# Layer normalization of two batches made from a transposed copy of x and broadcast rows of moments

## The chip, the cores and the metric

The kernel runs on one core of a Trainium2 chip, as one launch. The metric is device time in microseconds (us). The work of a core is spread over engines with an instruction queue each: TensorE (PE, matrix products and transposes), VectorE (DVE), ScalarE (ACT), GpSimd (POOL) and SyncE (SP), whose queue issues nearly all of this kernel's DMA transfers between DRAM and on-chip memory. Matrix results land in PSUM, everything else lives in SBUF; both have 128 partitions.

## What is computed

Two layers run over x, 4 batches of 512 rows with 256 columns, float32. Each has the same frame and its own mixer and feed-forward part:

```python
xn = _layernorm(x, axis=-1)
s = _L0_attn_ref(xn, ...)
g = _silu(_L0_ffn_ref(xn, L0_ffn_W1, L0_ffn_W2, L0_ffn_W3))
x = x + s * g
xn = _layernorm(x, axis=-1)
s = _L1_attn_ref(xn, L1_attn_qkv, L1_attn_o_proj, L1_attn_gamma, L1_attn_beta)
g = _silu(_L1_ffn_ref(xn, L1_ffn_W1, L1_ffn_W2, L1_ffn_W3))
x = x + s * g
```

`_layernorm` subtracts the mean of each row and divides by the root of its variance plus 1e-5. The first layer's mixer starts from a zero state, so it reduces to a matrix product, a root-mean-square normalization and a residual. The second layer's is causal attention with one head. The feed-forward part is

```python
up_gate = jnp.einsum('bsd,hd->bsh', x, W1)
up_lin = jnp.einsum('bsd,hd->bsh', x, W3)
hidden = jax.nn.silu(up_gate) * up_lin
hidden = fwht(hidden)
out = jnp.einsum('bsh,dh->bsd', hidden, W2)
```

with H = 1024 hidden columns; `fwht` is a Walsh-Hadamard transform of the hidden columns.

## The kernel before

**Products.** Every float32 operand of a product is split into a high part, which ACT casts (line 61), and a low part, which DVE subtracts (line 62). A product is then three: high by high, high by low, low by high (`mm3`, all issued at line 70). A contraction runs over partitions, so the products with xn need xn transposed: columns on partitions, rows along the free axis. The two halves of 128 columns are called k = 0 and 1.

**Stages of the first layer.** The loop from line 1014 goes over the four batches; the text calls its turns stages one to four, and their tiles carry f_0 to f_3. A stage is the feed-forward part of one batch (`ffn`, line 474): for each of 8 column blocks c, 24 products of 128x512 into two PSUM tiles `f_bgu` (`f_b` followed by the batch, from zero), silu on ACT (line 535), a multiply with the second tile on DVE (line 537, the gate product, `f_bh`), the split into `f_bhh` and `f_bhl`, and one block later 12 products of 128x256 with W2 into `f_bdn` (its parts are `w2h` and `w2l`; the transform is folded into them beforehand by `prep_w2`, whose products are `w2ps`).

**What runs beside a stage.** `Beside` (line 893) takes a list of tasks, made of steps, and spreads the steps over the 16 slots of a stage, in the order of the list. In the stage of batch b (from zero) the tasks are, in order:

- the gate of the batch before (`gate_all`, from stage two on): silu of `f_(b-1)dn`, times s, added to x;
- the mixer of this batch (`mixer`, line 725): products `o` of the transposed xn with a folded matrix, squares on ACT, then on DVE line 739, four scalings of `osb` and the sum at line 745;
- the layernorm of the next batch (`norm(0, b+1)`, line 438). `layernorm` makes statistics (four bn_stats, four bn_aggr, one addition on DVE, a power on POOL) and xn (four tensor_scalar). `transpose_half` (line 290) then has PE transpose four blocks of 128x128 for each k into a PSUM tile (`xt_btp`), and the split reads that tile: ACT casts the high part of 128x512, DVE subtracts the low one. The result, `xTs[0, b]`, is what the next stage's products and mixer read;
- preparation of the second layer: in stage two its W2 (`prep_w2`) and the attention weights (`prep_second`); in stages three and four `prep_s(q)`, line 327, for q = 0 to 3. It loads a block of weights (`sraw`, 512 KB on SP), makes four sums of it on DVE (`ssum`, 128x256 each), splits blocks and sums (128x768 and 128x1024) and writes them to DRAM, from where the second layer reads them.

Two batches of the second layer's normalization begin in these stages too: `norm(1, 0)` in stage three, between `prep_s(1)` and `prep_s(2)`, and parts of the first attention in stage four, ahead of `prep_s(3)`. `norm(1, b)` computes xn and the moments of xn (`moments`, line 256), has PE transpose the 8 columns of moments into rows (`mrp`), copies the rows on ACT, writes them to a DRAM tile (`there`) and reads them back broadcast over all partitions (`mrb`, [128, 2, 512]), both on SP. `Attention.xt` and `.scaled` (lines 759 and 780) use these rows: each row of the transposed tile has the mean row subtracted and is multiplied by the row of inverse deviations (`xf`, pieces of 128x512).

**Order.** In the stages a scheduler decides each engine's order from the order of the program, the dependences and explicit hints: `after(ins)` has what is issued in it stand behind instruction `ins`. `first["gate"]` is the last gate product so far, `first["scaled"]` the last tensor_scalar of the latest layernorm, `first["moments"]` the latest addition in `moments`; `line["last"]` is the last PE instruction. From the end of stage four on, PE's order is the program's: the last two `f_3dn` blocks stand behind `tq` (line 794, attention's query products, split into `tqh` and `tql`), then the second layer's first units with `v` (line 802), whose PSUM tile takes one of the three banks of the pool `ms`, which the transposes, `mrp`, `o`, `tq` and `w2ps` use in turn. SP carries the loads and stores in the order it is given, and an instruction that waits there holds all behind it.

**Buffers.** `t4` is a pool of ten 4 KB tiles per partition, shared by `osb`, `sraw`, `ssum`, `sp`, `mrb` and others; `x` has four slots, `xn` three, `xt` two.

Of the kernel before, what the change touches and what calls it, by code (L numbers as in the profile page):

```python
# [11 lines left out]
F32 = mybir.dt.float32  # L12
# [5 lines left out]
ALU = mybir.AluOpType  # L18
# [3 lines left out]
P = 128  # L22
D = 256
B = 4
S = 512
H = 1024
NH = H // P
NT = S // P
DS = 16
LN_EPS = 1e-5  # L30
# [5 lines left out]
def kernel(ctx: ExitStack, tc: tile.TileContext, a: dict, out: bass.AP):  # L36
    nc = tc.nc

    wp = ctx.enter_context(tc.tile_pool(name="weights", bufs=1))
    act = ctx.enter_context(tc.tile_pool(name="act", bufs=2))  # L40
    dram = ctx.enter_context(tc.tile_pool(name="dram", bufs=2, space=bass.MemoryType.DRAM))
    ps = ctx.enter_context(tc.tile_pool(name="ps", bufs=2, space=PSUM))

    def t4(name, shape, dt=F32):
        return act.tile(shape, dt, tag="t4", name=name, bufs=10)
# [10 lines left out]
    def psum(name, shape, tag="ms", bufs=3):  # L56
        return ps.tile(shape, F32, tag=tag, name=name, bufs=bufs)
# [8 lines left out]
    line = {"fixed": False, "last": None}  # L66
# [10 lines left out]
    def transpose(*args):  # L77
        return in_line(nc.tensor.transpose, *args)
# [15 lines left out]
    xs = {}  # L94
# [4 lines left out]
    def load_x(b, nt=NT, queues=(nc.sync,)):  # L99
        xs[b] = x_slot(f"x{b}", [P, NT, D])  # L100
        src = a["x"][b].rearrange("(t p) d -> p t d", p=P)
        for t in range(0, NT, nt):
            queue = queues[t // nt % len(queues)]
            queue.dma_start(xs[b][:, t : t + nt, :], src[:, t : t + nt, :])

    ident, had_f, mask = (wp.tile([P, P], F32, name=n) for n in ("ident", "had_f", "mask"))
# [146 lines left out]
        return hi, lo  # L253


    def moments(name, x, mr):

        st = act.tile([P, NT, 6], F32, tag="stats", name=f"{name}st", bufs=4)
        mv = act.tile([P, NT, 2], F32, tag="mv", name=f"{name}mv", bufs=4)
        for t in range(NT):  # L260
            nc.vector.bn_stats(st[:, t, :], x[:, t, :])
        for t in range(NT):
            nc.vector.bn_aggr(mv[:, t, :], st[:, t, :])
        nc.vector.tensor_copy(mr[:, 0, :], mv[:, :, 0])
        first["moments"] = nc.vector.tensor_scalar(mr[:, 1, :], mv[:, :, 1], LN_EPS, None, ALU.add)
        nc.gpsimd.tensor_tensor(mr[:, 1, :], mr[:, 1, :], mhalf, ALU.pow)

    def layernorm(name, x, y, groups=(NT,)):
# [38 lines left out]
    xns, xTs, mrs = {}, {}, {}  # L307

    def xt_pair(name):

        both = act.tile([P, 2, 2, S], F32R, tag="xt", name=name, bufs=2)
        return both[:, 0], both[:, 1]
# [14 lines left out]
    def prep_s(q):  # L327

        raw = t4(f"sraw{q}", [P, 4, D])
        nc.sync.dma_start(raw, a["w13_1"][q])  # L330
        yield
        sums = t4(f"ssum{q}", [P, 4, D])
        a11, a12, a22, a21 = (raw[:, i, :] for i in range(4))
        s1, s2, s3, s4 = (sums[:, i, :] for i in range(4))
        nc.vector.tensor_tensor(s1, a21, a22, ALU.add)
        nc.vector.tensor_tensor(s3, a11, a21, ALU.subtract)
        nc.vector.tensor_tensor(s2, s1, a11, ALU.subtract)
        nc.vector.tensor_tensor(s4, a12, s2, ALU.subtract)
        yield
        sdram[q] = there = [  # L340
            dram.tile([P, 7, D], F32, tag=f"s{i}", name=f"s{i}_{q}", bufs=4) for i in range(2)
        ]
        for at, n, src in ((0, 3, raw), (3, 4, sums)):
            parts = [t4(f"sp{at}_{i}_{q}", [P, n, D], F32R) for i in range(2)]
            split(src[:, :n, :], *parts)
            for i in range(2):
                nc.sync.dma_start(there[i][:, at : at + n, :], parts[i].bitcast(F32))
            yield
# [32 lines left out]
    def norm_first():  # L381
# [53 lines left out]
        first["norm"] = hi_, lo_  # L435
        yield

    def norm(layer, b):
        xn = act.tile([P, NT, D], F32, tag="xn", name=f"xn{layer}_{b}", bufs=3)
        xns[layer, b] = xn  # L440
        with after(first["gate"] if b > 1 - layer else None):
            first["scaled"] = layernorm(f"ln{layer}_{b}", xs[b], xn)
        yield
        if layer:


            mr = act.tile([P, 2, NT], F32, tag="mr", name=f"mr{b}", bufs=2)
            moments(f"ln2_{b}", xn, mr)
            yield
            o = psum(f"mrp{b}", [2 * NT, P], **DN[b == 0])  # L450
            transpose(o, mr.rearrange("p a t -> p (a t)"), ident)
            rows = act.tile([2 * NT, P], F32, tag="rows", name=f"rows{b}", bufs=1)
            with after(first["table"] if b else None):
                nc.scalar.copy(rows, o)
            there = dram.tile([2 * NT, P], F32, tag="rows", name=f"there{b}")
            nc.sync.dma_start(there, rows)
            mrb = t4(f"mrb{b}", [P, 2, S])
            nc.sync.dma_start(
                mrb, there.rearrange("(a t) p -> a (t p)", a=2).unsqueeze(0).to_broadcast([P, 2, S])
            )  # L460
            mrs[b] = mrb
            yield
            return
        hi, lo = xTs[0, b] = xt_pair(f"xt0_{b}")
        for k in range(2):
            o = transpose_half(f"xt0_{b}", xn, k)
            first["xt"] = line["last"]
            split(o, hi[:, k, :], lo[:, k, :])
            yield

    def after(ins):
        return tc.issue_after(ins.ins) if ins else nullcontext()
# [252 lines left out]
    def mixer(b):  # L725

        xn, xT, m = xns[0, b], xTs[0, b], first["m"]
        osb = t4(f"osb{b}", [P, NT, D])
        r = small(f"ssr{b}")
        junk = t2(f"junk{b}", [P, D])  # L730
        for i in range(2):
            o = psum(f"o0_{b}_{i}", [P, 2, D])
            for j in range(2):
                mm3(o[:, j, :], k_pairs(xT, sl(2 * i + j), m, ALLD))
            nc.scalar.copy(osb[:, 2 * i : 2 * i + 2, :], o)
            for t in (2 * i, 2 * i + 1):
                nc.scalar.activation(junk, osb[:, t, :], AF.Square, accum_out=r[:, t : t + 1])
            yield
        nc.vector.tensor_scalar(r, r, 1.0 / D, RMS_EPS, ALU.mult, ALU.add)
        nc.gpsimd.tensor_tensor(r, r, mhalf, ALU.pow)  # L740
        for t in range(NT):
            nc.vector.scalar_tensor_tensor(
                osb[:, t, :], osb[:, t, :], r[:, t : t + 1], nwb, ALU.mult, ALU.mult
            )
        nc.vector.tensor_tensor(xn, xn, osb, ALU.add)
        yield

    class Attention:
# [3 lines left out]
        def __init__(self, b):  # L752
            self.b, self.halves = b, []
# [171 lines left out]
    def call(f, *args):  # L925
        f(*args)
        yield


    NORM, MIXER, W2P = 3, 3, 12  # L930
# [27 lines left out]
    first = {"table": None}  # L958
# [52 lines left out]


    dn = None
    for b in range(B):
        tasks = []
        if b == 0:
            prep = prep_first()
            next(prep)
            tasks.append((prep, 12))
        if b:  # L1020
            tasks.append((call(gate_all, f"g0_{b - 1}", dn, xns[0, b - 1], xs[b - 1]), 1))
        tasks.append((mixer(b), MIXER))
        if b + 1 < B:
            if b:
                load_x(b + 1)
            if b == 2:
                tasks.append((prep_s(0), 4))
            tasks.append((norm(0, b + 1), NORM))
        if b == 0:
            early = w2_tile("early0"), w2_tile("early1")  # L1030
            spare = [
                [early[i][:, 2 * c : 2 * c + 2, :].rearrange("p a d -> p (a d)") for i in range(2)]
                for c in range(NH // 2)
            ]
        if b == 1:
            raw2_1 = load_w2(1)
            w2_1 = w2_tiles(1)
            tasks.append((prep_w2(1, raw2_1, w2_1, t4), W2P))
            tasks.append((prep_second(), 5))
        if b == 2:  # L1040
            tasks += [(prep_s(1), 4), (norm(1, 0), NORM), (prep_s(2), 4)]
        if b == 3:
            atts = [Attention(0)]
            at = atts[0]
            parts = run(at.xt_half, 0), run(at.xt_half, 1), at.xt, at.scaled, at.split_sums
            tasks += [(call(f), 1) for f in parts]
            norms = {1: norm(1, 1)}
            tasks.append((prep_s(3), 4))
        bg = Beside(*tasks)
        if b == 0:  # L1050
            dn = ffn("f0_0", xTs[0, 0], w13, w2, bg.slot, NH, spare, parts=2, behind=True)
        else:
            tail = [run(atts[0].tq, j) for j in range(2)] if b + 1 == B else []
            dn = ffn(f"f0_{b}", xTs[0, b], w13, w2, bg.slot, tail=tail)
        bg.finish()
# [36 lines left out]
    for b in range(B):  # L1092
        a, final = atts[b], b + 1 == B
# [113 lines left out]
```

## Time and profile before

| | |
|---|---|
| time, median of 3 runs | 358.37 us (358.14 to 358.87) |
| time of the profiled execution | 358.41 us |
| its span | 356.6 us |
| mean granted TensorE clock | 1.00 |
| busy: PE, DVE, ACT, POOL | 350.6, 287.1, 197.7, 20.8 us |
| instructions: PE, DVE, ACT, POOL | 2477, 598, 374, 22 |

The span is the time from the first to the last instruction that the profiler shows; the time of the execution has 1.8 us more around it. Stage one's products begin at 7.7 us, stage two's at 50.8, stage three's at 87.5, stage four's at 127.5, and the second layer starts at some 170.5. A busy engine is not an engine on the path: DVE and ACT are busy beside PE.

A line of a group or of a timeline gives the engine, the source line, the operation, the tile written and the tiles read, and the shapes; "x4" counts the instructions in it. Buffer numbers are left out of tile names, so the four batches' xn are all `xn`.

### The profile page before, as it was taken

What the parts mean: (1) busy time and instruction counts of PE and PEld (TensorE: products, weight loads), DVE (VectorE), ACT (ScalarE), POOL (GpSimd) and SP (SyncE); (2) the same over time, 40 slices, a digit from 0 to 9 for tenths busy, and PEclk for the clock granted to TensorE, in tenths of its full rate; (3) what the DMA queues carried; (4) which work ended last, traced back from release to release, by engine and by line L of the source; (5) the groups of instructions that cost most, each with busy time, mean ns of one, the idle gap of its engine ahead of it and who ended that gap; (6) DMA issues with size and microseconds to landing.
All of it is one profiled execution on the core that took longest, in us unless ns stands there. A gap on an engine that the chain in (4) does not pass through costs nothing.

```text
span 356.6 us, 6276 instructions
## 1 busy us (share of the span) xinstructions
PE 350.6 (98%) x2477; PEld 326.8 (92%) x2477; DVE 287.1 (81%) x598; ACT 197.7 (55%) x374; POOL 20.8 (6%) x22
## 2 busy tenths in 40 slices
PE   7999999999999999999999999999999999999995
PEld 6878998888988898888999999999999999999994
DVE  6899659998579938998887957989679897678646
ACT  4666166265463425674467755586555676556443
POOL 2000110300020110100110001100011000000000
PEclk9999999999999999999999999999999999999999
DMA  7935000301044306656257145661554635445401
GB/s 242 339 97 200 2 1 2 117 0 61 0 164 172 139 38 239 249 180 193 109 208 265 37 170 209 219 235 79 206 188 171 221 163 206 143 151 190 196 2 59
DMA packets 16284, 52.25 MB, mean 147 GB/s; under 512 B 1632, under 2 KB 7936, under 8 KB 16256
## 3 DMA queue, kind: packets, MB, share of 16 engines
q1 hardware_dynamic: 15968, 51.60, 40.5%
q8 instruction: 19, 0.31, 0.4%
q10 hardware_dynamic: 288, 0.26, 0.2%
q14 instruction: 9, 0.07, 0.1%
HBM read 42.40 MB, written 9.45 MB: 145 GB/s over the span
## 4 chain that ended last, share of the span: by engine, by line
PE 97%; DVE 1%; DMA 1%; ACT 0%; issue 0%
PE f_0dn L70 6%; PE f_1dn L70 6%; PE f_2dn L70 6%; PE f_0gu L70 6%; PE f_1gu L70 6%; PE f_2gu L70 6%; PE f_3gu L70 6%; PE f_3dn L70 6%; PE sc L70 4%; PE pv L70 4%; PE o L70 3%; PE v L70 3%; PE tq L70 3%; PE w2ps L70 1%; PE pt L70 1%; PE f_3gu1g L70 1%
## 5 line engine op out<-in xcount | busy, mean ns | idle before, releaser
L70 PE MATMUL f_3gu<-xt,w 128*128 128x512 f32 x96 | 25.0, 396 | 0.0
L70 PE MATMUL f_2gu<-xt,w 128*128 128x512 f32 x96 | 24.8, 395 | 0.0
L70 PE MATMUL f_1gu<-xt,w 128*128 128x512 f32 x96 | 24.8, 395 | 0.0
L70 PE MATMUL f_0gu<-xt,w 128*128 128x512 f32 (+1 forms) x108 | 24.3, 378 | 0.0
L70 PEld LDWEIGHTS f_0gu<-xt,w 128*128 128x128 f32 x108 | 18.4, 188 | 4.4 <-issue 1.0
L70 PEld LDWEIGHTS f_1gu<-xt,w 128*128 128x128 f32 x96 | 17.0, 188 | 3.1
L70 PEld LDWEIGHTS f_2gu<-xt,w 128*128 128x128 f32 x96 | 17.0, 188 | 3.0
L70 PEld LDWEIGHTS f_3gu<-xt,w 128*128 128x128 f32 x96 | 17.0, 188 | 2.9
L61 ACT CAST f_2hh<-f_2h 128x512 fp32r<-128x512 f32 x16 | 10.0, 622 | 15.4 <-DVE f_2h L537 12.3
L70 PE MATMUL f_3dn<-w2l,f_3hh 128*128 128x256 f32 x64 | 17.7, 281 | 0.0
L70 PE MATMUL f_3dn<-w2h,f_3hh 128*128 128x256 f32 x64 | 17.7, 281 | 0.0
L70 PE MATMUL f_1dn<-w2l,f_1hh 128*128 128x256 f32 x64 | 17.7, 281 | 0.0
L70 PE MATMUL f_2dn<-w2h,f_2hh 128*128 128x256 f32 x64 | 17.7, 282 | 0.0
L70 PE MATMUL f_1dn<-w2h,f_1hh 128*128 128x256 f32 x64 | 17.6, 280 | 0.0
L70 PE MATMUL f_2dn<-w2l,f_2hh 128*128 128x256 f32 x64 | 17.6, 280 | 0.0
L70 PE MATMUL f_3dn<-w2h,f_3hl 128*128 128x256 f32 x64 | 17.0, 281 | 0.0
L70 PE MATMUL f_1dn<-w2h,f_1hl 128*128 128x256 f32 x64 | 17.0, 281 | 0.0
L70 PE MATMUL f_2dn<-w2h,f_2hl 128*128 128x256 f32 x64 | 16.7, 281 | 0.0
L61 ACT CAST f_3hh<-f_3h 128x512 fp32r<-128x512 f32 (+1 forms) x17 | 10.0, 594 | 10.3 <-DVE f_3h L537 6.1
L61 ACT CAST f_1hh<-f_1h 128x512 fp32r<-128x512 f32 x16 | 9.9, 621 | 9.7 <-DVE f_1h L537 6.6
L62 DVE TENSOR_TENSOR f_2hl<-f_2h,f_2hh 128x512 fp32r<-128x512 f32 x16 | 10.9, 684 | 4.5 <-ACT f_2hh L61 4.5
L62 DVE TENSOR_TENSOR f_3hl<-f_3h,f_3hh 128x512 fp32r<-128x512 f32 (+1 forms) x17 | 11.0, 654 | 3.7 <-ACT f_3hh L61 3.6
(487 smaller groups left out, 1146.1 us busy)
## 6 DMA issues: line engine op xcount, KB each, us to landing
sw<-s SPq DMA_DIRECT2D x32, 896.0 KB, 5.8
s<-sp SPq DMA_DIRECT2D x8, 512.0 KB, 4.1
s<-sp SPq DMA_DIRECT2D x8, 384.0 KB, 2.8
w2raw<-in_w SPq DMA_DIRECT2D x4, 512.0 KB, 4.8
sraw<-in_w SPq DMA_DIRECT2D x4, 512.0 KB, 4.2
mrb<-there SPq DMA_DIRECT2D x4, 512.0 KB, 3.7
w13raw<-in_w SPq DMA_DIRECT2D x3, 512.0 KB, 6.2
x<-in_x SPq DMA_DIRECT2D x3, 512.0 KB, 3.5
```

The costliest lines, as they stand in the source:

```text
L61: h = nc.scalar.copy(hi, src)
L62: return h, engine.tensor_tensor(lo, src, hi.bitcast(F32), ALU.subtract)
L70: ins = call(*args, **kwargs)
```

## The change

The layernorm of the third and the fourth batch in the first layer goes another way. A class `FromTransposed` holds its three parts, for b = 2 and 3:

- `begin`, the last task of stage one for the third batch and of stage two for the fourth: loads x of the batch, a second copy of it that the host has laid out transposed (`xT2`, `xT3`, [128, 2, 512]), and makes the moments on DVE and POOL;
- `rows`, in the stage ahead of the batch's own (stage two for the third batch, stage three for the fourth), directly behind the gate of the batch before: PE's transpose of the moments' 8 columns, the copy of the rows, the write to DRAM and the broadcast read;
- `steps`, in the place of `norm(0, b)`: xn by four tensor_scalar as before, since the mixer and the residual need it; then the transposed xn, from the transposed x by a subtraction of the mean row and a multiplication by the row of inverse deviations, each one DVE instruction of 128x1024 whose row operand is broadcast over k; the high part by one ACT cast of 128x1024, and the low part by one DVE subtraction of 128x1024, in place of the PE transposes and the two splits of 128x512 from PSUM.

The write and the broadcast read are taken out of `norm` into `spread`, which both use. `norm(0, 1)` and `norm(1, 0)` change a hint: they now stand behind `first["gate"]` too, where they had no hint. `moments` can leave `first["moments"]` as it is.

```diff
--- before.py
+++ after.py
@@ -253,7 +253,7 @@
         return hi, lo
 
 
-    def moments(name, x, mr):
+    def moments(name, x, mr, pin=True):
 
         st = act.tile([P, NT, 6], F32, tag="stats", name=f"{name}st", bufs=4)
         mv = act.tile([P, NT, 2], F32, tag="mv", name=f"{name}mv", bufs=4)
@@ -262,7 +262,9 @@
         for t in range(NT):
             nc.vector.bn_aggr(mv[:, t, :], st[:, t, :])
         nc.vector.tensor_copy(mr[:, 0, :], mv[:, :, 0])
-        first["moments"] = nc.vector.tensor_scalar(mr[:, 1, :], mv[:, :, 1], LN_EPS, None, ALU.add)
+        ins = nc.vector.tensor_scalar(mr[:, 1, :], mv[:, :, 1], LN_EPS, None, ALU.add)
+        if pin:
+            first["moments"] = ins
         nc.gpsimd.tensor_tensor(mr[:, 1, :], mr[:, 1, :], mhalf, ALU.pow)
 
     def layernorm(name, x, y, groups=(NT,)):
@@ -435,10 +437,67 @@
         first["norm"] = hi_, lo_
         yield
 
+    def spread(name, rows):
+
+        there = dram.tile([2 * NT, P], F32, tag="rows", name=f"there{name}")
+        nc.sync.dma_start(there, rows)
+        mrb = t4(f"mrb{name}", [P, 2, S])
+        nc.sync.dma_start(
+            mrb, there.rearrange("(a t) p -> a (t p)", a=2).unsqueeze(0).to_broadcast([P, 2, S])
+        )
+        return mrb
+
+    class FromTransposed:
+
+        def __init__(self, b):
+            self.b = b
+
+        def begin(self):
+            b = self.b
+            load_x(b)
+            self.raw = t4(f"xTraw{b}", [P, 2, S])
+            nc.sync.dma_start(self.raw, a[f"xT{b}"])
+            self.mr = act.tile([P, 2, NT], F32, tag="mr", name=f"mr0_{b}", bufs=2)
+            with after(first["scaled"] if b == 2 else first["gate"]):
+                moments(f"ln0_{b}", xs[b], self.mr, pin=False)
+            yield
+
+        def rows(self):
+            b = self.b
+            o = psum(f"mrp0_{b}", [2 * NT, P])
+            with after(line["last"]):
+                transpose(o, self.mr.rearrange("p a t -> p (a t)"), ident)
+            rows = act.tile([2 * NT, P], F32, tag="rows", name=f"rows0_{b}", bufs=1)
+            nc.scalar.copy(rows, o)
+            self.mrb = spread(f"0_{b}", rows)
+
+        def steps(self):
+            b, mr = self.b, self.mr
+            xns[0, b] = xn = act.tile([P, NT, D], F32, tag="xn", name=f"xn0_{b}", bufs=3)
+            with after(first["gate"]):
+                for t in range(NT):
+                    nc.vector.tensor_scalar(
+                        xn[:, t, :], xs[b][:, t, :], mr[:, 0, t : t + 1], mr[:, 1, t : t + 1],
+                        ALU.subtract, ALU.mult,
+                    )
+            yield
+            hi, lo = xTs[0, b] = xt_pair(f"xt0_{b}")
+            raw = self.raw
+            for i, op in enumerate((ALU.subtract, ALU.mult)):
+                row = self.mrb[:, i, :].unsqueeze(1).to_broadcast([P, 2, S])
+                with after(first["gate"]):
+                    nc.vector.tensor_tensor(raw, raw, row, op)
+            nc.scalar.copy(hi, raw)
+            yield
+            nc.vector.tensor_tensor(lo, raw, hi.bitcast(F32), ALU.subtract)
+            yield
+
     def norm(layer, b):
         xn = act.tile([P, NT, D], F32, tag="xn", name=f"xn{layer}_{b}", bufs=3)
         xns[layer, b] = xn
-        with after(first["gate"] if b > 1 - layer else None):
+        with after(first["gate"] if b or layer else None):
             first["scaled"] = layernorm(f"ln{layer}_{b}", xs[b], xn)
         yield
         if layer:
@@ -452,13 +511,7 @@
             rows = act.tile([2 * NT, P], F32, tag="rows", name=f"rows{b}", bufs=1)
             with after(first["table"] if b else None):
                 nc.scalar.copy(rows, o)
-            there = dram.tile([2 * NT, P], F32, tag="rows", name=f"there{b}")
-            nc.sync.dma_start(there, rows)
-            mrb = t4(f"mrb{b}", [P, 2, S])
-            nc.sync.dma_start(
-                mrb, there.rearrange("(a t) p -> a (t p)", a=2).unsqueeze(0).to_broadcast([P, 2, S])
-            )
-            mrs[b] = mrb
+            mrs[b] = spread(b, rows)
             yield
             return
         hi, lo = xTs[0, b] = xt_pair(f"xt0_{b}")
@@ -1011,6 +1064,7 @@
 
 
     dn = None
+    others = {b: FromTransposed(b) for b in (2, 3)}
     for b in range(B):
         tasks = []
         if b == 0:
@@ -1019,13 +1073,15 @@
             tasks.append((prep, 12))
         if b:
             tasks.append((call(gate_all, f"g0_{b - 1}", dn, xns[0, b - 1], xs[b - 1]), 1))
+            if b + 1 in others:
+                tasks.append((call(others[b + 1].rows), 0))
         tasks.append((mixer(b), MIXER))
         if b + 1 < B:
-            if b:
+            if b and b + 1 not in others:
                 load_x(b + 1)
             if b == 2:
                 tasks.append((prep_s(0), 4))
-            tasks.append((norm(0, b + 1), NORM))
+            tasks.append((others[b + 1].steps() if b + 1 in others else norm(0, b + 1), NORM))
         if b == 0:
             early = w2_tile("early0"), w2_tile("early1")
             spare = [
@@ -1046,6 +1102,8 @@
             tasks += [(call(f), 1) for f in parts]
             norms = {1: norm(1, 1)}
             tasks.append((prep_s(3), 4))
+        if b + 2 in others:
+            tasks.append((others[b + 2].begin(), 0))
         bg = Beside(*tasks)
         if b == 0:
             dn = ffn("f0_0", xTs[0, 0], w13, w2, bg.slot, NH, spare, parts=2, behind=True)
@@ -1174,6 +1232,8 @@
     flat = lambda n: v[f"L0_attn_{n}"].reshape(4, P, DS)
     arrays = {
         "x": v["L0_attn_x"],
+        "xT2": v["L0_attn_x"][2].T.reshape(2, P, S).transpose(1, 0, 2),
+        "xT3": v["L0_attn_x"][3].T.reshape(2, P, S).transpose(1, 0, 2),
         "ident": np.eye(P, dtype=np.float32),
         "hadamard": (_sylvester(P) / np.sqrt(H)).astype(np.float32),
         "mask": np.where(np.tril(np.ones((P, P), bool)), 0.0, NEG).astype(np.float32),
```

## The prediction

> **What bounds the kernel now.** I read the page first, for who is busy and who ends the chain of waits:
>
> ```profile
> span 356.6 us, 6276 instructions
> ...
> PE 350.6 (98%) x2477; PEld 326.8 (92%) x2477; DVE 287.1 (81%) x598; ACT 197.7 (55%) x374; POOL 20.8 (6%) x22
> ...
> PE 97%; DVE 1%; DMA 1%; ACT 0%; issue 0%
> ```
>
> PE is the whole chain, and the list of waits shows PE waiting for another engine only at the start (1.5 and 0.4 us). So a product taken off PE is worth its pitch (start to start), and any new PE wait costs its full length. The profiled execution took 358.41 us (the median of the runs is 358.37): span 356.6 and 1.8 around it. My sum starts from 358.41.
>
> Second, PE's timeline around the removed transposes, here the fourth batch's (columns: start, duration):
>
> ```profile
> 119.59 0.38 PE L70 MATMUL xt_3tp<-ident,xn 128*128 128x128 f32 x2
> 119.73 0.36 PE L70 MATMUL f_2dn<-w2h,f_2hh 128*128 128x256 f32 x1
> 119.93 0.28 PE L70 MATMUL f_2dn<-w2l,f_2hh 128*128 128x256 f32 x1
> ...
> 120.29 0.82 PE L70 MATMUL xt_3tp<-ident,xn 128*128 128x128 f32 x6
> 120.86 1.41 PE L70 MATMUL f_2gu<-xt,w 128*128 128x512 f32 x5
> 122.11 0.28 PE L70 MATMUL f_2dn<-w2h,f_2hl 128*128 128x256 f32 x1
> ```
>
> Starts matter here, not durations: two transposes hold PE 0.14 us, six hold it 0.57, and the product behind each group takes longer than its like (0.20 against 0.12; five wide ones 1.25 against 5 x 0.232 = 1.16).
>
> Third, how full DVE is, by stage (columns: window, its us, DVE busy and count, PE clock, DMA share, GB/s), since DVE gets the new work:
>
> ```profile
> 57.00:84.00 27.00, 26.70 (x52) 1.00 0.18 59
> 84.00:104.00 20.00, 12.59 (x21) 1.00 0.07 27
> 104.00:125.70 21.70, 21.40 (x60) 1.00 0.47 171
> 125.70:133.80 8.10, 1.99 (x4) 1.00 0.11 43
> 143.50:169.40 25.90, 23.93 (x49) 1.00 0.61 201
> ```
>
> DVE is full in three stretches, with holes of some 7 and 6 us between them. Fourth, DVE and the SP queue in the places where something could become late:
>
> ```profile
> 70.84 1.22 DVE L745 TENSOR_TENSOR xn<-xn,osb 128x1024 f32<-128x1024 f32 x1
> 73.18 0.69 DVE L62 TENSOR_TENSOR f_1hl<-f_1h,f_1hh 128x512 fp32r<-128x512 f32 x1
> 167.15 0.69 DVE L62 TENSOR_TENSOR tql<-tq,tqh 128x512 fp32r<-128x512 f32 x1 [0.46 <-ACT tqh L61]
> 167.91 0.66 DVE L62 TENSOR_TENSOR f_3hl<-f_3h,f_3hh 128x512 fp32r<-128x512 f32 x1
> ```
>
> ```profile
> 80.91 0.33 SPq L330 DMA_DIRECT2D sraw<-in_w  x1
> ...
> 129.94 0.33 SPq L456 DMA_DIRECT2D there<-rows  x1
> 131.17 0.34 SPq L458 DMA_DIRECT2D mrb<-there  x1
> 131.57 0.42 SPq L330 DMA_DIRECT2D sraw<-in_w  x1
> ...
> 136.54 0.43 DVE L335 TENSOR_TENSOR ssum<-sraw 128x256 f32<-128x256 f32 x1 [0.38 <-DMA sraw<-in_w]
> ```
>
> The write of rows lands within 1.23 us, mrb holds the queue 0.40, and the sraw behind it took 4.9 us to reach DVE.
>
> **PE: what goes and what comes.** Fourth batch: 0.14 + 0.57 + 0.08 + 0.09 = 0.88. Third batch, by the same reading at 71.88 to 74.62: 0.14 + 0.57 + 0.07 + 0.09 = 0.87. Each batch gains one 8-column transpose of moments: the mrp at 129.36 and the slower o product behind it cost 0.10 together. Net -1.75 + 0.20 = **-1.55 us**. Every PE instruction ahead of a late one moves up too, so the lead must be given back before anything is lost.
>
> A duration tempts here: the Trainium skill ("TensorE: Matmul & The Clock Gate", Part 4: PE-mode transpose) gives about 275 ns for a transpose in a kernel's context. The row's duration, 272 ns, agrees, but the pitch is 95 ns; by 275 ns the 16 would be worth 4.4 us, an estimate from the page, and the verdict below would turn round.
>
> **DVE, ACT, POOL per batch.** New on DVE: two tensor_tensor of 128x1024 over two SBUF tiles, 1.13 us of pitch each (the row at 70.84, followed by one at 71.97). A broadcast operand is not in the trace at this width; bounds are 1.13 and 2 x 0.60 = 1.20 (two 128x512 pieces, as xf<-xf,mrb at 0.60); I take 1.13. The final subtract is one of 1.13 instead of two of 0.60. The moments (4 stats 1.31, 4 aggregates 0.32, small ones 0.15) move one batch ahead, into the holes at 44 and 88 us, at no cost there: that work ran in full stretches before. ACT: one cast of 1.05 for two of 0.59, and a copy of rows of 0.25; ACT is 55% busy. POOL's power moves with the moments, long before its reader. Two x^T loads of 512 KB and two mrb transfers run where the DMA share is 0.07 to 0.31, hidden. The earlier pin of the second batch's layernorm in stage one falls in a stretch where DVE then idles 5.07 us (before L739): nothing.
>
> **First new wait: column block 3 of stage two.** In the built order of DVE, between f_1h0 and the f_1hl of column block 3, new are: a gate add 0.60, subtract 1.13, multiply 1.13, second w2l as well as the first 1.20, last subtract 1.13: 5.19. Gone from there: stats 1.31, aggregates 0.32, one small 0.07: 1.70. f_1h0 itself starts earlier (PE's order now finishes f_1gu0 without o products between: 14 wide pitches after 50.8, plus silu 0.60, gives 54.9 for 56.09). So f_1hl ends at 73.86 + 5.19 - 1.70 - 1.19 + 0.4 (it waits for ACT's f_1hh0 behind the new rows copy) = 76.6. PE read it at 76.48; now -0.87 + 0.10 for the transposes and +0.46 for a w2ps pair moved ahead: 76.2. With its high half, cast just before, I take **+0.65** (bounds 0 and 1.2, the latter if f_1h0 is not early).
>
> **Second and third: SP's order.** sraw (prep_s) now stands behind there, mrb of the fourth batch. Its transpose of rows comes after f_1dn's last product and 18 f_2gu products: 95.74 + 1.40 = 97.1. Copy and ACT's queue 0.6, there 1.23, mrb 0.40, landing 4.2 to 4.9: DVE gets sraw0 at 103.6 to 104.3 where it read it at 98.27. DVE idles in that hole, and the queue up to the moments of layer two (13 x 0.60, 6 x 1.13, 2 x 0.87, 8 x 0.33, osb 1.58, two xn 2.60, stats 2.62, small 0.85 = 26.6) ends near 130.6, for 125.7. (These prices reproduce before's own 104.36 to 125.71 to 0.1 us.) The row transpose mrp0 stands in PE's new order after f_3gu2's tenth product: 141.67 - 36 x 0.118 + 0.93 - 0.9 (PE's lead) = 137.4, where it ran at 129.36. Then sraw2 is issued at 139.6 instead of 131.57 and usable at 139.6 + 4.9 = 144.5 instead of 136.5. The five-step sums of prep_s(2) (3.3 us) fall out of a hole into the last full stretch.
>
> From 144.5 DVE has, up to the last f_3hl: 18 x 0.60, 12 x 0.33, 2 x 0.87, 3 x 1.13, osb 1.58, stats 1.31, small 0.23 = 23.05, and 2.0 of waits as before's stretch had: 169.55. PE wants it at 169.38 - 0.9 = 168.5: **+1.15**. Behind it, now ahead of tql: 0.56 of small ones, ACT's cast of sums (1.0 waited), 1.13, xn 1.30, two gate products 1.20, tql 0.68: it ends at 175.4, for 167.84. v's second half takes the PSUM bank that tql frees; PE reached it at 173.39, now 173.39 - 0.9 + 1.15 = 173.6: **+1.8**. Behind it in PE's fixed order everything waits.
>
> The Trainium skill ("DMA: Bandwidth & Descriptors", Anatomy of one DMA) puts about 2.0 us of fixed cost on a transfer, where the write of rows here was followed after 1.23. By 2.0 sraw2 would come 0.8 later and the sum be 0.8 higher, an estimate; the row is of this very transfer, so it decides.
>
> Sum: -1.55 + 0.65 + 1.15 + 1.8 = +2.05; 358.41 + 2.05 = **360.5 us**.
>
> **Rivals.** (a) The holes absorb all: 358.41 - 1.55 = 356.9. It needs tql no more than 4.0 us later than 167.84 (173.39 - 1.55 - 167.84); I get 7.5, so sraw2 would have to be usable by 141. For it: PE never waited before, with 2.6 us to spare at f_1hl and 5.5 at v. Against: the SP order. 10%. (b) Only the wait in stage two comes, the tail stays hidden: 358.41 - 1.55 + 0.65 = 357.5. Same condition on tql, at 3.4 us more given the lead that is left. 6%. (c) Only part of the tail: sraw2 lands after 4.2 and DVE's waits are shorter by 1: 358.41 - 1.55 + 0.65 + 0 + 1.2 = 358.7. 8%. (d) More: transfers or POOL's power (1.01 to 1.91 in its rows) slower beside the fuller DVE, prep_s late by another 2 us, which comes through whole: 362.5. 16%. That the change does not do what it says is excluded by the built order: 16 transposes are gone, two row transposes there. The forecast keeps 60%.
>
> **Range and chances.** A difference of 0.2% (0.7 us) is about what can be told here from none. Low end: between (c) and (a) with the unknown 0 to 1.2 of stage two, 358.6; high end (d), 362.6. Slower by over 0.2% (above 359.1): forecast, (d) and a little of (c): 0.80. Within: most of (c) and half of (b): 0.09. Faster: (a), the rest of (b): 0.11.
>
> **What would show it.** Eight transposes less in each of two stages, PE about 0.8 us ahead at f_2gu's start; tensor_tensor of 128x1024 on raw at 1.2 us; sraw's first issue near 99 and third near 140; DVE idle just before both; PE idle some 0.65 at f_1dn near 76, and 1 to 3 us in all at f_3dn and v near 169 to 175, released by DVE; layer two otherwise unchanged. Wrong if PE shows no wait at v, or if sraw's third issue comes before 136.

## The result and the profile after

The changed kernel takes 361.23 us (median of 6 runs, 360.86 to 361.84) against 358.34 for the kernel before: a ratio of 1.0079, interval 1.0068 to 1.0091, so 2.9 us slower. The profiled execution took 360.86, 2.45 more than the 358.41 of the one before; the traces below explain those 2.45. The profiled run was the fastest of the six, and what the other five lost beyond it is in no trace.

The page of the changed kernel, the lines on spans, engines and the chain that ended last:

```profile
span 359.1 us, 6272 instructions
...
PE 350.6 (98%) x2463; PEld 325.3 (91%) x2463; DVE 291.1 (81%) x602; ACT 198.4 (55%) x374; POOL 18.8 (5%) x22
...
PE 93%; DVE 4%; ACT 1%; issue 0%; DVEq 0%
```

PE has 14 instructions fewer, as the change says, but the chain is no longer all PE: 4% of it is DVE. PE's list of waits for other engines names three that weren't there (us in all, times, the longest):

```profile
PE v L70 <- DVE tql L62: 1.6, 1, 1.6
...
PE f_3dn L70 <- DVE f_3hl L62: 0.7, 1, 0.7
PE f_1dn L70 <- DVE f_1hl L62: 0.2, 1, 0.2
```

The list shows only what is left after the modelled end of the product before. The starts say more. PE's timeline at the three places:

```profile
72.88 1.55 PE L70 MATMUL f_1gu<-xt,w 128*128 128x512 f32 x6
74.49 0.39 PE L70 MATMUL f_1dn<-w2h,f_1hh 128*128 128x256 f32 x1
74.72 0.28 PE L70 MATMUL f_1dn<-w2l,f_1hh 128*128 128x256 f32 x1
...
75.06 1.58 PE L70 MATMUL f_1gu<-xt,w 128*128 128x512 f32 x6
76.83 0.38 PE L70 MATMUL f_1dn<-w2h,f_1hl 128*128 128x256 f32 x1 [0.19 <-DVE f_1hl L62]
77.05 0.28 PE L70 MATMUL f_1dn<-w2h,f_1hh 128*128 128x256 f32 x1
...
168.50 0.28 PE L70 MATMUL f_3dn<-w2l,f_3hh 128*128 128x256 f32 x1
169.51 0.38 PE L70 MATMUL f_3dn<-w2h,f_3hl 128*128 128x256 f32 x1 [0.72 <-DVE f_3hl L62]
169.73 0.28 PE L70 MATMUL f_3dn<-w2h,f_3hh 128*128 128x256 f32 x1
...
172.93 0.87 PE L70 MATMUL f_0gu0z<-tb,sw 128*128 128x256 f32 x6
175.41 0.50 PE L70 MATMUL v<-wvoh,xgh 128*128 128x256 f32 x2 [1.62 <-DVE tql L62]
```

Six wide products take 6 x 0.232 = 1.39, so the two starts in stage two come 0.22 and 0.38 late; after 168.50 the next was due at 168.62 and began 0.89 later; after 172.93 plus 6 x 0.118 it was due at 173.64 and began 1.77 later. Each first product after a wait also held PE 0.22 to 0.23 (74.49 to 74.72, 76.83 to 77.05, 169.51 to 169.73) where its like hold it 0.12: a wait costs its length and about 0.1 more.

DVE by the same windows as in the prediction:

```profile
57.00:84.00 27.00, 25.64 (x42) 1.00 0.26 79
84.00:104.00 20.00, 13.04 (x27) 1.00 0.16 53
104.00:125.70 21.70, 20.99 (x41) 1.00 0.47 171
125.70:133.80 8.10, 6.55 (x21) 1.00 0.16 65
...
143.50:169.40 25.90, 23.34 (x47) 1.00 0.67 221
```

The hole behind stage three's full stretch is mostly filled: 6.55 us busy between 125.7 and 133.8, for 1.99 before. DVE idles later instead, 3.87 us up to 142.52 and 1.32 up to 144.53, when the load comes. DVE's and SP's timelines where things became late:

```profile
69.68 1.22 DVE L491 TENSOR_TENSOR xTraw<-xTraw,mrb 128x1024 f32<-128x1024 f32 x1
70.82 0.68 DVE L590 TENSOR_TENSOR f_1h<-f_1h,f_1gu 128x512 f32<-128x512 f32 x1
...
76.09 0.69 DVE L62 TENSOR_TENSOR f_1hl<-f_1h,f_1hh 128x512 fp32r<-128x512 f32 x1
...
104.71 0.43 DVE L337 TENSOR_TENSOR ssum<-sraw 128x256 f32<-128x256 f32 x1 [1.15 <-DMA sraw<-in_w]
...
131.74 0.16 DVE L265 TENSOR_SCALAR mr<-ln_0mv 128x4 f32<-128x4 f32 x1
...
144.53 0.42 DVE L337 TENSOR_TENSOR ssum<-sraw 128x256 f32<-128x256 f32 x1 [1.32 <-DMA sraw<-in_w]
...
168.80 0.65 DVE L62 TENSOR_TENSOR f_3hl<-f_3h,f_3hh 128x512 fp32r<-128x512 f32 x1
...
172.17 1.38 DVE L286 TENSOR_SCALAR xn<-x,ln_1mv,ln_1r 128x256 f32<-128x256 f32 x4
173.47 1.29 DVE L767 TENSOR_TENSOR g_3g<-g_3g,xn 128x512 f32<-128x512 f32 x2
174.67 0.68 DVE L62 TENSOR_TENSOR tql<-tq,tqh 128x512 fp32r<-128x512 f32 x1
```

```profile
98.15 0.29 SPq L443 DMA_DIRECT2D there<-rows  x1
99.42 0.33 SPq L445 DMA_DIRECT2D mrb<-there  x1
99.80 0.42 SPq L332 DMA_DIRECT2D sraw<-in_w  x1
...
137.98 0.28 SPq L443 DMA_DIRECT2D there<-rows  x1
139.20 0.32 SPq L445 DMA_DIRECT2D mrb<-there  x1
139.57 0.43 SPq L332 DMA_DIRECT2D sraw<-in_w  x1
```

The load for prep_s(0) left SP at 99.80 for 80.91, the one for prep_s(2) at 139.57 for 131.57, and DVE got them at 104.71 and 144.53, each after an idle wait. The last `f_3hl` ends at 169.45 (168.57 before) and the first `tql` at 175.35 (167.84 before), behind the four xn and the two gate products that DVE did after it in the kernel before. The write of rows that holds the second load back waits for PE, not for DVE: DVE has the moments of norm(1, 0) ready at 131.90 and POOL their power at 133.05, but PE comes to their transpose only at 137.39, where it stands in PE's built order behind 34 products of `f_3gu` (behind six in the kernel before, at 129.36).

### The profile page after: what moved, and what is told of

Read it like the earlier page. It is cut to its first block, busy times and chain, and to the rows that moved or that the text cites. A ratio compares the mean times of both kernels' runs of the same rounds, so it can differ in the third digit from the quotient of the medians.

```text
span 359.1 us, 6272 instructions
## 1 busy us (share of the span) xinstructions
PE 350.6 (98%) x2463; PEld 325.3 (91%) x2463; DVE 291.1 (81%) x602; ACT 198.4 (55%) x374; POOL 18.8 (5%) x22
## 4 chain that ended last, share of the span: by engine, by line
PE 93%; DVE 4%; ACT 1%; issue 0%; DVEq 0%
PE f_0dn L70 6%; PE f_2dn L70 6%; PE f_0gu L70 6%; PE f_3gu L70 6%; PE f_2gu L70 6%; PE f_1dn L70 6%; PE f_1gu L70 5%; PE f_3dn L70 5%; PE sc L70 4%; PE pv L70 4%; PE o L70 3%; PE v L70 3%; PE tq L70 2%; PE warm L70 1%; PE pt L70 1%; PE w2ps L70 1%
## 5 line engine op out<-in xcount | busy, mean ns | idle before, releaser
L70 PE MATMUL f_0dn<-w2h,f_0hh 128*128 128x256 f32 x48 | 13.6, 283 | 0.0
```

Source lines behind the costliest of these rows:

```text
L70: ins = call(*args, **kwargs)
```

## The experiments

Each is compared with the kernel before on the same chip. "Net" is the shift of PE's last product against the kernel before in the two profiled executions, less the shift that the execution already had when the first stage's products began (these starts differ by up to 0.6 from one execution to the next).

**Both weight loads ahead on SP.** Nothing else is changed:

```diff
+            if b == 2:
+                s0 = prep_s(0)
+                tasks.append((call(next, s0), 1))
             if b + 1 in others:
                 tasks.append((call(others[b + 1].rows), 0))
...
-                tasks.append((prep_s(0), 4))
+                tasks.append((s0, 3))
...
-            tasks += [(prep_s(1), 4), (norm(1, 0), NORM), (prep_s(2), 4)]
+            s2 = prep_s(2)
+            tasks += [(prep_s(1), 4), (call(next, s2), 1), (norm(1, 0), NORM), (s2, 3)]
```

> The changed kernel with two loads moved ahead on SP and nothing else: the weights of prep_s(0) are loaded before the rows of the fourth batch are spread, those of prep_s(2) before norm(1, 0) is issued. DVE, ACT and PE do the same instructions. Theory (the sums of prep_s come late because their loads stand behind the two writes and broadcast reads of rows, and fall into the last full stretch of DVE): DVE reads sraw of q = 0 near 86 and of q = 2 before 128, PE's waits at the last f_3dn (0.88 by pitch) and at v (1.78) both go, with the 0.1 that the first product after each loses; stage two's wait stays. PE's lead over before stands at 0.76 ahead of the tail, so 358.4 - 0.76 = 357.6, at most 358.0. Rival (DVE simply has too much to do in all): the same work is there, both waits stay, 361.2. Rival (the added transfers take bandwidth): they are all still there, 360 or more.

Measured: 357.98 (357.57 to 358.61, 10 runs), ratio 0.9991 (0.9982 to 1.0001); net -0.6. SP's and DVE's timelines of this kernel:

```profile
81.58 0.33 SPq L332 DMA_DIRECT2D sraw<-in_w  x1
98.73 0.29 SPq L443 DMA_DIRECT2D there<-rows  x1
...
121.20 0.38 SPq L332 DMA_DIRECT2D sraw<-in_w  x1
...
138.76 0.28 SPq L443 DMA_DIRECT2D there<-rows  x1
```

```profile
100.63 0.41 DVE L337 TENSOR_TENSOR ssum<-sraw 128x256 f32<-128x256 f32 x1
...
169.21 1.25 DVE L62 TENSOR_TENSOR tql<-tq,tqh 128x512 fp32r<-128x512 f32 x2
```

The sums begin at 100.63 and 138.12, in DVE's holes again (98.27 and 136.54 in the kernel before), though not near 86 and before 128 as expected. With the same 602 instructions on DVE, both low parts of tq now end by 170.46, and PE's only new wait is stage two's. 3.25 us of the time come back. The rivals that blame the amount of DVE's work or the added transfers, both unchanged here, fall as causes by themselves; that SP's order is needed for the tail's waits is shown. Each edit also lets the scheduler build DVE's and PE's orders anew (here the low parts of tq stand ahead of the gate products again), so an experiment shows the edit with the orders that follow from it. The order at the end of DVE is tried by itself below.

**One load alone.** The two halves of the edit above, each by itself, first that of prep_s(2), then that of prep_s(0).

> The changed kernel with one load moved ahead on SP: that of prep_s(2), before norm(1, 0); that of prep_s(0) stays behind the spread of the fourth batch's rows. Theory (both late loads count): the sums of q = 2 (0.34 to 0.87 each, 3.3 us) leave the last full stretch, tql is in time and the wait at v (1.78 and 0.1) goes; but with q = 0 still late these sums lengthen DVE's queue in stage three, the moments and rows of norm(1, 0) come 1 to 1.5 later and so does the last f_3hl: the wait at f_3dn grows from 0.9 to some 1.7: 361.2 - 1.9 + 0.8 = 360.1 (359.2 to 360.6). Rival (only the last load counts): both tail waits go, 358.0 as with both loads ahead. Rival (neither): 361.2.

> The changed kernel with the load of prep_s(0) alone moved ahead of the spread of the fourth batch's rows; that of prep_s(2) stays behind the rows of norm(1, 0). Theory (both count): DVE's queue in stage three is shorter by some 1 to 2, the rows of norm(1, 0) reach SP only 0.5 earlier since PE's order holds their transpose, sraw of q = 2 is issued near 139; v's wait goes or shrinks since DVE's order in the tail is met earlier, f_3dn's wait stays at 0.3 to 0.9 and some of it comes in the second layer's first units: 359.2 to 360.4. Rival (only the last load counts): 361.2. Rival (only the first counts): 358.0.

Measured: 359.85 (359.60 to 360.19; ratio 1.0042, 1.0027 to 1.0057) and 359.91 (359.64 to 360.18; ratio 1.0041, 1.0027 to 1.0055). With prep_s(2) ahead v's wait is gone and the start of `f_3dn` is 1.61 late (0.89 in the changed kernel). With prep_s(0) ahead `f_3dn` is 0.43 late, some 0.4 and 0.24 come in the second layer's first units, and some 0.5 in starts of tq between 164.8 and 166.6. So both loads count. Alone they bring 1.38 and 1.32, together 3.25: with either load late DVE is still behind in the tail, and what differs is which product waits for it.

**One batch alone.** `others` holds only batch 2 (the third), or only batch 3 (the fourth, whose moments then wait for `first["gate"]`).

> Only the third batch goes the new way; the fourth keeps norm(0, 3). Theory: stage two as in the changed kernel (waits of 0.22 and 0.34 and 0.1 of restart), half of the saving on PE (0.78), and nothing in the tail, since sraw of q = 0 stands behind no spread of rows and is issued near 81: 358.34 - 0.78 + 0.67 = 358.2. Rival (the hint that norm(1, 0) now has, which is in this kernel too, makes the tail late by itself): waits of some 2.7 in the tail, 360.9.

> Only the fourth batch goes the new way. Theory: no wait in stage two (f_1hl of column block 3 ends at 73.9 as before), half of the saving (0.78), sraw of q = 0 issued near 98 and of q = 2 near 139, and so waits in the tail, at most those of the changed kernel (2.66 and 0.2 of restarts), fewer if the 0.6 that stage two no longer loses lets DVE catch up: 358.3 to 360.4. Rival (each batch brings half of the loss): 359.8, with waits in both places.

Measured: 359.12 (358.86 to 359.75; ratio 1.0020, 1.0011 to 1.0030) and 359.89 (359.85 to 360.22; ratio 1.0042, 1.0027 to 1.0057). The third batch alone shows the waits of stage two (0.22 and 0.34) and nothing over 0.3 in the tail; still it took 0.9 more than expected, of which its profiled execution shows 0.2 to 0.3 in starts of `f_3dn` and the rest isn't in it. It has the changed hint too, and the load of prep_s(2) leaves SP at 136.84; the kernel before with that hint alone (next experiment: 136.62) loses 0.2 there too. The fourth alone shows none in stage two and 0.46 at `f_3dn`, then 0.39 and 0.26 in the second layer's first units. Its rival had the time (359.8), but not the places. The tail's loss belongs to the fourth batch, as expected; the two sum to 2.2, less than the 2.9 of both.

**The hint.** First the changed kernel with norm's old hint, then the kernel before with the new one:

```diff
-        with after(first["gate"] if b or layer else None):
+        with after(first["gate"] if b > 1 - layer else None):
```

> The changed kernel with norm's old hint, so that norm(0, 1) and norm(1, 0) don't stand behind the gate. Theory (the lateness of the rows of norm(1, 0) is what counts at the end): their transpose on PE returns from 137.4 to about 130.5, sraw of q = 2 is issued near 133, and the tail's waits go (2.66 and 0.2), but the layernorm and moments of the second layer (1.30, 1.31, 1.31 and some 0.6) come back into DVE's full stretch of stage three and may have PE wait there for up to their length less the slack: 358.4 to 360.9. Rival (the hint does nothing here, DVE's order being bound elsewhere): 361.2 with the same three waits.

> The kernel before with the changed hint in norm alone (norm(0, 1) and norm(1, 0) behind the gate). Theory: the hint moves the transposed rows of norm(1, 0) from 129.4 to about 134 and sraw of q = 2 from 131.6 to about 136.5, and DVE without the new work takes that: no PE wait, 358.3 (358.1 to 358.6). Rival (the hint makes the tail late by itself): waits at f_3dn or v, 359 to 361.

Measured: 360.79 (360.64 to 361.81; ratio 1.0074, 1.0056 to 1.0091), and 358.88 (358.25 to 359.05; ratio 1.0010, 1.0001 to 1.0019). With the old hint the rows are transposed at 131.52 and the load of prep_s(2) is issued at 133.91. The tail's waits are gone and stand in stage three instead, as PE's list of waits shows (stage two's stay):

```profile
PE f_2dn L70 <- DVE f_2hl L62: 2.1, 2, 1.4
```

With the new hint on the kernel before, SP issues the load of prep_s(2) at 136.62, 5 us later than without, and the profiled execution (358.46) has no wait over 0.15. Six of the 10 runs took 358.85 or more, and the median is 0.3 outside the expectation; where these lose it is in no trace. The hint takes up slack of the tail and costs 0.04 to 0.7 by the interval, but not 2.9.

**The order on DVE at the end.** The gate of the fourth batch and the next layernorm behind the low parts of tq:

```diff
+            first["tql"] = split(o, self.tqs[0][:, j, :], self.tqs[1][:, j, :])[1]
-            split(o, self.tqs[0][:, j, :], self.tqs[1][:, j, :])
...
     line["fixed"] = True
+    first["gate"] = first["moments"] = first["tql"]
     gate_all("g0_3", dn, xns[0, 3], xs[3])
```

> The changed kernel with a hint: the gate of the fourth batch and the layernorm of norm(1, 1) stand on DVE behind the low parts of tq. SP's order and all work stay. Theory (DVE is some 5 us behind, so an order only says who waits for it): tql ends near 172 instead of 175.3 and v's wait of 1.78 goes, but what now stands behind it (gate products 1.2, xn 1.3, sums) is late for the second layer's first units, and PE waits there for 2 to 4 us in all: 361.0 to 363.0. Rival (the fault is only that tql stands behind those): 361.2 - 1.9 = 359.3.

Measured: 362.35 (362.16 to 362.61), ratio 1.0111 (1.0096 to 1.0126). PE's list of waits and DVE's timeline:

```profile
PE f_0gu1g L70 <- issue: 3.2, 1, 3.2
...
PE mrp L70 <- POOL mr L268: 0.7, 1, 0.7
```

```profile
171.19 1.29 DVE L62 TENSOR_TENSOR tql<-tq,tqh 128x512 fp32r<-128x512 f32 x2 [0.24 <-ACT tqh L61]
```

The two waits of the tail are gone, since the last `f_3hl` (ending at 168.28) and tql are in time, and a longer one stands at `f_0gu1g`, which takes the bank that a late DVE instruction (L716, ending at 182.21) frees 0.1 before. DVE is behind, whoever is served first; the rival falls.

**Less work on DVE.** One of the two row operations is left out:

```diff
-            for i, op in enumerate((ALU.subtract, ALU.mult)):
+            for i, op in enumerate((ALU.subtract,)):
```

> The changed kernel without the multiplication by the row of inverse deviations (the transposed xn of the third and fourth batch isn't scaled): 1.13 less on DVE in stage two and again in stage three; loads, rows, transfers and SP's order are those of the changed kernel. Theory, in the strict form that SP's order alone sets the tail: stage two's wait of 0.66 goes (f_1hl 1.13 earlier), the rows of norm(1, 0) move by no more than PE, and the tail stays: 360.3 to 360.7. Theory, in the form that DVE's queue of stage three sets when the moments of norm(1, 0) are ready, and these when SP gets to prep_s(2): the tail shrinks by 1.13 or more as well: 358.4 to 359.6.

Measured: 358.96 (358.75 to 359.55), ratio 1.0019 (1.0009 to 1.0028). No wait in stage two; 0.37, 0.41 and 0.20 in the tail. The load of prep_s(2) leaves SP at 138.56, only 1.0 earlier, and yet 2.3 us come back for 2.26 of DVE work. So the strict form (SP's order alone) falls too. The other form has the time right, but its path isn't what the trace shows: POOL has the moments at 131.68 and PE comes to their transpose at 135.95, so here too the rows wait for their place on PE, not for DVE. With the difference in the start of the two executions taken off, the transpose is 1.8 us earlier, 0.8 by stage two's wait and 0.9 by the four products of `f_3gu` that it now stands ahead of. DVE's order is another too: the low parts of tq (170.11 and 171.42) stand ahead of the gate products and of three of the four xn. What is shown is that SP's order decides when the sums can start, and that with 2.26 less to do DVE no longer falls as far behind; how much of the 2.3 is the work and how much the orders built with it is open.

**Stage two's wait.** One number in the pacing:

```diff
-            tasks.append((prep_w2(1, raw2_1, w2_1, t4), W2P))
+            tasks.append((prep_w2(1, raw2_1, w2_1, t4), 4))
```

> The changed kernel with one number changed: the preparation of the second layer's W2 counts as 4 steps instead of 12 in stage two's list, so that its later steps slide towards the stage's end, where DVE has idle time. Theory (stage two's wait is DVE's queue alone, the tail's waits are another matter): f_1hl of column block 3 ends near 73.9 again instead of 76.8, the waits of 0.22 and 0.34 with 0.1 of restart go, and PE is 0.8 ahead of before at stage three's start. The tail's waits hang on SP and DVE, which follow PE's stage three, so they stay at about 0.9 and 1.8: 361.2 - 0.7 = 360.5 (360.2 to 360.9). Rival (a lead gained early is given back in the tail, whose end DVE sets by the clock): 361.2.

Measured: 359.72 (359.48 to 361.45), ratio 1.0049 (1.0033 to 1.0065); PE was some 0.6 to 0.8 ahead at the end of stage two, so its wait is gone, and the tail's two (0.89, 1.79) stayed. The gain is 1.5, where 0.7 was expected. Of the difference 0.25 is a delay in the second layer (see below) that isn't there here; the rest, some 0.5, is in no trace and less than the runs of the changed kernel differ by (1.0). Its profiled execution was the slowest of the seven (361.45) and shows why the place is fragile. DVE, then PE:

```profile
105.99 0.42 DVE L337 TENSOR_TENSOR ssum<-sraw 128x256 f32<-128x256 f32 x1 [3.14 <-DMA sraw<-in_w]
...
109.79 0.68 DVE L590 TENSOR_TENSOR f_2h<-f_2h,f_2gu 128x512 f32<-128x512 f32 x1
```

```profile
110.53 1.67 PE L70 MATMUL f_2gu<-xt,w 128*128 128x512 f32 x6 [1.19 <-DVE f_2h L590]
```

The late load, issued at 99.39, took 6.6 us to reach DVE here (4.9 in the changed kernel); DVE held its queue for it, the gate product behind came late, and PE waited for the bank that this frees.

**Both cures.** The two loads ahead and the pacing together:

> Both cures at once: the two weight loads ahead of the spreads of rows on SP, and the preparation of W2 counted as 4 steps. Theory: no PE wait is left in stage two or in the tail, so what remains is the work taken off PE, 16 transposes less two of 8 columns (-1.55 by the pitches; 0.76 was seen of one batch with its row): 358.35 - 1.5 = 356.8 (356.5 to 357.3). Rival (a lead on PE is given back at the next place where DVE, a PSUM bank or a weight load is just in time, as the two cures were only seen one by one): 357.7 or more. Rival (the fuller queues cost the products time everywhere): 358.

Measured: 357.17 (356.80 to 357.35), ratio 0.9962 (0.9949 to 0.9976): faster than the kernel before by 1.2 us and than the changed kernel by 4.1. PE's waits and the chain:

```profile
PE warm L70 <- DVE zr L994: 1.5, 1, 1.5
```

```profile
PE 98%; DVE 1%; ACT 0%; issue 0%
```

The only wait left is the one at the start, which the kernel before has too; net is -1.5. What the change takes off PE is worth 1.5 us once nothing is late.

## Why the prediction held, step by step

The direction and the mechanism were right, and the time (360.5 forecast, 361.23 measured) lies in the range. By the profiled executions the forecast was +2.05 and the trace shows +2.45:

| term | predicted | measured | from |
|---|---|---|---|
| PE work taken off | -1.55 | -1.5 | the kernel with both cures, net |
| stage two, column block 3 | +0.65 | +0.8 | starts: 0.22 + 0.38, and 0.1 after each |
| last f_3dn block | +1.15 | +1.0 | 0.89 + 0.1 |
| v behind tql | +1.8 | +1.9 | 1.77 + 0.1 |
| second layer, tq | none | +0.25 | below |

Pitch against duration: the 1.5 decides for the pitch of 0.095. The Trainium skill ("TensorE: Matmul & The Clock Gate", Part 4: PE-mode transpose) gives some 275 ns for one, which agrees with the row's duration, but as a price of PE time it would have made this gain 4.4.

That the three rows of waits agree so well is in part luck. By length alone the waits came to 3.26 (0.22 + 0.38, 0.89, 1.77) where 3.6 was forecast, and the 0.1 of each restart, which the forecast left out, made up 0.4: two errors that cancel. One of them is in the working itself: for the last f_3dn block it gives 169.55 less 168.5, that is 1.05, and the sum has 1.15.

DVE's prices: a broadcast row operand cost nothing extra, 1.14 from start to start (69.68 to 70.82) where 1.13 to 1.20 was the bound. `f_1hl` ended at 76.78 (predicted 76.6), the last `f_3hl` at 169.45 (169.55), `tql` at 175.35 (175.4). The queue of stage three ended later than forecast, with the moments ready at 131.90 for 130.6, but nothing hung on it: the row transpose behind them ran at 137.39 (137.4), by its place in PE's order.

SP's order: the third `sraw` was issued at 139.57 (139.6) and usable at 144.53 (144.5); the first went out at 99.80 and reached DVE at 104.71 (103.6 to 104.3: the landing took 4.9, the upper bound, and the rows were 0.4 later). The write of rows was followed after 1.27 and 1.22. The Trainium skill ("DMA: Bandwidth & Descriptors", Anatomy of one DMA) has about 2.0 us fixed for a transfer, fitted for transfers that GpSimd issues; these are issued by SP, and the two rows don't show it.

What else was off is small. Of the signs named, PE 0.8 us ahead at f_2gu's start doesn't fit the forecast's own sum, which gives the lead back in stage two (-0.78 and +0.65); in the trace PE is level with the kernel before there, and 0.8 ahead only at the first `f_3gu` (126.68 for 127.50). The prediction took the second layer as unchanged; there PE lost another 0.25 at the second batch's tq products:

```profile
206.22 0.75 PE L70 MATMUL tq<-xgh,wqkh 128*128 128x512 f32 x2
206.81 0.64 PE L70 MATMUL tq<-xgh,wqkl 128*128 128x512 f32 x2
207.28 0.71 PE L70 MATMUL tq<-xgl,wqkh 128*128 128x512 f32 x2
207.84 0.63 PE L70 MATMUL tq<-xgh,wqkh 128*128 128x512 f32 x2
```

```profile
206.75 0.68 DVE L62 TENSOR_TENSOR xgl<-xg,xgh 128x512 fp32r<-128x512 f32 x1
```

The first and the third pair take 0.59 and 0.56 where the kernel before had 0.46 and 0.46: the second high part that the first pair reads ends on ACT at 206.41, and the second low part that the third reads on DVE at 207.43, each inside its pair. The remaining 0.4 between the profiled run and the median wasn't foreseen and isn't explained by a trace; the loads that DVE now waits for directly, as in the slowest execution of the pacing experiment, are a candidate, not a finding.

The rivals: that the holes absorb all (356.9), or all but stage two (357.5), did not come about because of SP's order, as argued; with the loads ahead they are near what is measured (357.17 with both cures, 357.98 with the loads alone). Rival (b)'s condition was misread: by the prediction's rows tql could be 4.65 us late (173.39 - 0.9 - 167.84), not 3.4; it was 7.5 late, beyond either. The hint was costed at nothing in stage one and its other half, norm(1, 0), was not priced on its own; it moves the rows of norm(1, 0) from about 130 to 135 even without the rest, and so holds a part of the slack that the tail then lacked.

## What to carry to other kernels

Work moved off the bound engine must be followed to the in-order queue that feeds its replacement: here a write of rows and the broadcast read that waits for it, put ahead of a weight load in two places, cost more than 16 transposes saved, and issuing the loads first turned a loss of 2.9 us into a tie, with one pacing number a gain of 1.2. An engine that is 81% busy on average can be full in the one stretch that counts, so read its windows, and give new work a place where it idles. Moving a late result ahead in the order of an engine that is behind only named another victim here.

## What the runs showed of the hardware

A PE wait cost about 0.1 us beyond its length: the first 128x256 product after it held PE 0.22 to 0.23 instead of 0.12, at all the places above. And one weight load of 512 KB, issued in the same place, took 4.9 us to its reader in the changed kernel's execution and 6.6 in that of the pacing experiment, where PE then lost 1.5 us at `f_2gu` (1.35 late, and 0.1).
